# A Mamba stage and a 4-bit feed-forward stage on one core: sums of W_out for two time blocks moved in among the last scans

## The chip, the cores and the metric

The kernel runs on one core of one Trainium2 chip. The metric is the time of one execution on the device, in microseconds (us). The engines are named as the profile names them: PE multiplies matrices (its weight loads are PEld), DVE and POOL work on vectors, ACT computes functions and copies, SP only starts DMA transfers. PE sums into PSUM, which has eight banks of 128 x 512 float32; everything else lies in SBUF.

## What is computed

The input x has 8192 tokens of 512 features. Cut to what matters here:

```python
h = _layernorm(x) * (1 + ca) + sa
x = x + ga * mamba(h)                  # ends in: y = (scan + xc * D) * silu(z);  return y @ W_out.T
h = _layernorm(x) * (1 + cb) + sb
x = x + gb * ffn(h)                    # silu(q(h) @ q(Wg).T) * (q(h) @ q(Wu).T), then q(.) @ q(W_down).T
```

Here q rounds each group of 16 numbers to a 4-bit grid with a scale of its own; 1408 is the inner width of the feed-forward part. In the Mamba part a scan runs over time for each of 1024 channels and 16 states.

## The kernel before, in words

**Two stages, one after the other.** The Mamba stage takes about the first 3780 us, the feed-forward stage the rest.

**Mamba stage.** Time is cut into NC = 16 chunks of T = 512 tokens, a chunk into NJ = 4 time blocks of 128; the 1024 channels into ND = 8 channel blocks of P = 128. Two channel blocks (DH = 2) make a "half", of which there are NH = 4. The scans set the beat: a chunk is 64 slots, a slot is one scan (L547 on DVE, 128 x 1024) for one channel block and two states. The scanned states are multiplied by C, into hc by DVE (L565) or, for 5 slots of 16, into hp by POOL (L560). PE transposes these products and adds them up in the PSUM tile y (L438, `add_y`). The pool of hc has two buffers, and so has that of hp: a new one needs the y adds of the one before last.

The other work of the Mamba stage stands beside the scans by hand: `TABLE` (L577 to L617) gives each step a time in quarters of a slot, counted from the start of its chunk. Each slot has four moments (BEGIN, MID, GAP, END), `at` files a step under a slot and a moment, and `run` issues what is filed. Order on each engine is then the order of issue (`manual_schedule`). The steps at the end of a chunk are: `gate` (L450: z times y, DVE), `gate_t` (L456: PE turns the gated z of a channel block into a PSUM tile pgt), `gate_out` (L463: ACT copies it to xc, the eight of which are the input of W_out), `out_0` and `out_1` (L469: PE sums one time block po over channel blocks 0 to 3, then 4 to 7, four matmults each, 512 columns wide), `out_keep` (L482: ACT copies po; L485: it is stored to mo, for the last chunk from ACT's queue). For all chunks but the last these steps lie in the next chunk's slots; for the last one they come after all scans, in a plain loop over the slots that are left.

In PSUM the stage has a pool "mm" (one tile of one bank; pgt and po both live there), "cv" (one bank, used by the convolution), "y" (one tile of two banks) and "da" (two tiles of two banks): all eight banks.

**Feed-forward stage.** It goes by blocks of 512 tokens (n), each with four "heads" of 128 tokens. `load` (L963, L965) fetches mo and x of a head; the x tiles (h_t) have four buffers, so that of head 4 waits for PE's turn of head 0. `head` does the norm (POOL adds at L976, DVE L28 to L37, POOL L981 and L982) and the rounding to 4 bits (DVE L71 to L79, ACT L83 and L85, DVE L89 to L92, POOL L97). `turn` (PE L1002, ACT L1010) transposes a head into xqT. `up` (L1043) makes the gate and up products pg and pu, 11 pairs for each block, with L1048 (ACT), L1049 and L1050 (DVE) behind; it needs the turns of all four heads. `quantize` rounds their result, back through L1063. `down` (L1077) multiplies by W_down, and L1083 and L1084 finish a head. During the first two blocks, the four row blocks of W_down (wraw) are rounded too (`quantize_down`), transposed by PE (L1002) and copied by ACT into wd (L1033).

For the first two blocks of this stage no order is written by hand: the framework's scheduler puts the instructions of every engine in an order of its own, and it takes in what the Mamba stage left open (the tail's instructions are ordered together with the heads'). From the third block on the order is written by hand again.

Of the kernel before, what the change touches and what calls it, by code (L numbers as in the profile page):

```python
# [8 lines left out]
F32 = mybir.dt.float32  # L9
# [4 lines left out]
PSUM = bass.MemoryType.PSUM  # L14
DRAM = bass.MemoryType.DRAM

P = 128
# [91 lines left out]
def mamba_then_fp4_ffn(  # L109
# [25 lines left out]
    ND = DI // P  # L135
    NF = FF // P
    T = 512
    NJ = T // P
    NC = L // T
    NH = 4  # L140
    DH = ND // NH
# [28 lines left out]
    with ExitStack() as ma:  # L170
# [24 lines left out]
        SLOT_C = NH * SLOT_S  # L195
        NSLOT = NC * SLOT_C
        hT, xcs, bcd, dbcs, deltas, dus, zs, ys, bct, xts, pend = ({} for _ in range(11))
# [4 lines left out]
        def at(slot, moment, fn, *args):  # L202


            events.setdefault((slot, moment), []).append((fn, args))

        def run(slot, moment):
            for fn, args in events.pop((slot, moment), ()):
                fn(*args)

        pools = {}

        def run_all(slot):
            for moment in range(4):
                run(slot, moment)

        def mm_tile(name):
            return pools["mm"].tile([P, T], F32, tag="mm", name=name)
# [232 lines left out]

        def gate_t(k, d):
            h, i = divmod(d, DH)
            pg = mm_tile(f"pgt_{k}_{h}_{i}")
            for j in range(NJ):
                nc.tensor.transpose(  # L456
                    pg[:, j * P : (j + 1) * P], zs[k, h][:, j, i * P : (i + 1) * P], ident
                )
            pend["pg", k, h, i] = pg
# [2 lines left out]
            h, i = divmod(d, DH)  # L462
            nc.scalar.activation(xcs[k, h * DH + i], pend.pop(("pg", k, h, i)), AF.Copy)  # L463

        def out_mm(k, j, half):
            if half == 0:
                pend["po", k, j] = mm_tile(f"po_{k}_{j}")
            for d in range(half * (ND // 2), (half + 1) * (ND // 2)):
                nc.tensor.matmul(  # L469
                    pend["po", k, j], lhsT=xcs[k, d][:, j * P : (j + 1) * P], rhs=w_o[:, d, :],  # L470
                    start=(d == 0), stop=(d == ND - 1),
                )

        def out_0(k, j):
            out_mm(k, j, 0)

        def out_1(k, j):
            out_mm(k, j, 1)

        def out_keep(k, j):  # L480
            po = xp.tile([P, DM], F32, tag="x", name=f"po_{k}_{j}")
# [52 lines left out]
        def unit(slot):  # L534
# [90 lines left out]
            "skip": (skip_act, skip),  # L625
            "gate": (gate,),
            "gate_t": (gate_t, gate_out),
            "out": (out_0, out_1, out_keep),
        }
        for k in range(NC):  # L630
            for name, fns in steps.items():
                if k == 0 and name in ("norm", "conv", "x_proj"):
                    continue
                for m, times in enumerate(TABLE[name]):
                    for fn, time in zip(fns, times):
                        if k == 1 and name == "norm":
                            time -= 4 * (6 if m > 1 else 4)
                        if k == 0 and name in ("prep", "du") and time < 0:
                            time = min(time, 4 * -3 + GAP)
                        slot, moment = divmod(time, 4)  # L640
                        at(k * SLOT_C + slot, moment, fn, k, m)

# [2 lines left out]
        with tc.tile_pool(name="modp", bufs=1, side="right") as mp, tc.tile_pool(  # L647
            name="rawp", bufs=3, side="right"
        ) as rp, tc.tile_pool(name="qp", bufs=2, side="right") as qp, tc.tile_pool(
            name="xnp", bufs=3, side="right"  # L650
        ) as xnp, tc.tile_pool(name="qsm", bufs=3, side="right") as qsm, tc.tile_pool(
            name="p1", bufs=1, space=PSUM
        ) as p1, tc.tile_pool(name="p2", bufs=2, space=PSUM) as p2, tc.tile_pool(
            name="p3", bufs=3, space=PSUM
# [7 lines left out]
            class Work:  # L662


                @staticmethod
                def tile(shape, dtype, tag, name):
                    full = (xnp if tag == "xn" else qp).tile([P, 2 * DM], dtype, tag=tag, name=name)
                    return full[:, : shape[1]]
# [172 lines left out]
            for d in range(ND):  # L841
                h = 7 + 5 * d // 2
# [11 lines left out]
            for n, idx in enumerate((2, 5, 3, 4)):  # L854
                h = 8 + 6 * n
# [17 lines left out]
        own = dict(reuse_waits="tile")  # L873
        with ExitStack() as sa_:
# [10 lines left out]
            last = max(events)[0]  # L885
# [15 lines left out]
                    for moment in (MID, GAP, END):  # L901
                        run(slot, moment)

        for slot in range(NSLOT, last + 1):
            run_all(slot)
        order.close()


# [3 lines left out]
    with ExitStack() as fa:  # L912
# [261 lines left out]
        for n in range(2, NQ):  # L1174
# [3 lines left out]
            for q in range(NS):  # L1178
# [6 lines left out]
                else:  # L1185
                    f = q if q < split else q - NJ
                    c, i = divmod(f, FPB)
# [61 lines left out]
```

## Time and profile before

| what | us |
|---|---|
| median of 3 runs | 5715.73 |
| lowest and highest run | 5714.27, 5717.09 |
| the profiled execution | 5718.11 |
| its span in the trace | 5716.0 |
| PE busy | 5229.2 (91%) |
| DVE busy | 4963.9 (87%) |
| POOL busy | 4049.8 (71%) |
| ACT busy | 3215.3 (56%) |

Times below are counted from the start of the span of the profiled execution. A row of the timeline gives start, length, engine, line, operation, output and inputs, their sizes, and how many instructions (x) it holds; in brackets stands how long the engine had been idle before it, and what ended that. A matmult of 512 columns leaves two records, so x8 is four matmults. The granted clock is the share of its full speed that PE's clock was given.

### The profile page before, as it was taken

Reading aid. Unit: us, or ns where it says so; the run is one execution under the profiler, and the core shown is the slowest. Engines: PE = TensorE matmul, PEld = TensorE weight load, DVE = VectorE, ACT = ScalarE, POOL = GpSimd, SP = SyncE. Lnnn points to the kernel's source line nnn. Section 1 sums busy time; section 2 is a strip of 40 time slices with the busy share of each in tenths; the row PEclk is TensorE's granted clock in tenths of the full one; section 3 lists DMA queues with packets and bytes.
Section 4 is the critical chain, followed back from the end, with each engine's and each line's share of the span. In section 5 each row is a group of like instructions: output and inputs, shape, how many; then the busy total and the mean of one; then the engine's idle time right before and its main releaser. Section 6 shows DMA issues by size and latency. Waiting matters only on the chain. (4 is left out here: it accounts for less than half of the span.)

```text
span 5716.0 us, 59762 instructions
## 1 busy us (share of the span) xinstructions
PE 5229.2 (91%) x19844; PEld 3067.9 (54%) x19844; DVE 4963.9 (87%) x4003; ACT 3215.3 (56%) x7319; POOL 4049.8 (71%) x2548
## 2 busy tenths in 40 slices
PE   7789889889899898898998998778999999999999
PEld 4566565556565565565666655543444444444444
DVE  7899999999999999999999999988688788877885
ACT  6677786777777777777777776632122212221221
POOL 4899999999999999999999999973222233223320
PEclk9899999999999999999999999889999999999999
DMA  5444454454544444445445444540100010000100
GB/s 182 150 157 158 159 161 155 154 167 153 166 156 156 158 154 160 160 161 159 162 153 163 155 157 152 162 157 13 33 32 23 24 33 30 24 24 30 33 13 15
DMA packets 221996, 659.50 MB, mean 115 GB/s; under 512 B 24915, under 2 KB 40403, under 8 KB 221686
## 3 DMA queue, kind: packets, MB, share of 16 engines
q1 hardware_dynamic: 221110, 654.63, 35.2%
q8 instruction: 156, 2.56, 0.2%
q14 instruction: 154, 1.26, 0.1%
q10 hardware_dynamic: 576, 1.05, 0.0%
HBM read 615.22 MB, written 40.38 MB: 115 GB/s over the span
## 5 line engine op out<-in xcount | busy, mean ns | idle before, releaser
L509 POOL TENSOR_TENSOR db<-bc,du 128x1022 f32<-128x1022 f32 x1024 | 2388.7, 2356 | 26.6 <-DVE da L547 22.6
L547 DVE TENSOR_TENSOR_SCAN da<-da,db 128x1024 f32<-128x1024 f32 x704 | 1609.9, 2287 | 101.0 <-ACT da L522 89.2
L522 ACT ACTIVATE da<-delta,na 128x512 f32<-128x512 f32 x2048 | 1412.3, 690 | 90.1 <-DVE hp L547 62.1
L565 DVE TENSOR_TENSOR hc<-da,bc 128x1024 f32<-128x1024 f32 x704 | 861.3, 1223 | 95.3 <-PE y L438 46.0
L438 PE MATMUL y<-ident,hc 128*128 128x128 f32 x5632 | 766.9, 286 | 162.4 <-DVE hc L565 106.5
L438 PEld LDWEIGHTS y<-ident,hc 128*128 128x128 f32 x5632 | 672.9, 147 | 340.1 <-DVE hc L565 159.8
L97 POOL TENSOR_TENSOR xn<-xn,sc 128x1536 f32<-128x1536 f32 (+2 forms) x80 | 199.8, 2497 | 859.9 <-DVE xn L92 852.5
L560 POOL TENSOR_TENSOR hp<-hp,bc 128x1024 f32<-128x1024 f32 x320 | 754.0, 2356 | 25.6
L547 DVE TENSOR_TENSOR_SCAN hp<-da,db 128x1024 f32<-128x1024 f32 x320 | 730.0, 2281 | 44.4 <-ACT da L522 38.7
L1043 PE MATMUL pu<-xqT,wu 128*128 128x512 f32 x1408 | 635.6, 594 | 10.0 <-DVE g L1049 10.0
L1043 PE MATMUL pg<-xqT,wg 128*128 128x512 f32 x1408 | 635.3, 593 | 1.2 <-ACT xqT L1010 0.7
L83 ACT ACTIVATE a<-xn 128x512 f32<-128x512 f32 (+2 forms) x144 | 145.7, 1012 | 871.7 <-DVE xn L79 834.9
L1077 PE MATMUL po<-wd,hT 128*128 128x512 f32 x1408 | 609.8, 594 | 2.0 <-DVE hT L1063 2.0
L280 PE MATMUL cv<-hT,w_in 128*128 128x512 f32 x1024 | 498.7, 633 | 32.2 <-ACT hT L273 16.0
L412 PE MATMUL pz<-w_in,hT 128*128 128x256 f32 x2048 | 497.9, 399 | 27.3 <-DVE z L427 22.0
L308 PE MATMUL cv<-raw,taps 128*128 128x512 f32 x1024 | 467.9, 600 | 5.6 <-ACT taps L294 5.1
L469 PE MATMUL po<-w_o,xc 128*128 128x512 f32 x1024 | 463.2, 598 | 4.0 <-ACT po L482 3.3
L412 PEld LDWEIGHTS pz<-w_in,hT 128*128 128x128 f32 x2048 | 405.5, 203 | 97.4 <-DVE z L427 26.4
L1043 PEld LDWEIGHTS pu<-xqT,wu 128*128 128x128 f32 x1408 | 267.6, 191 | 347.0 <-issue 324.3
L545 ACT ACTIVATE state<-da 128x2 f32<-128x2 f32 x703 | 118.1, 168 | 595.6 <-DVE hc L565 594.4
L1077 PEld LDWEIGHTS po<-wd,hT 128*128 128x128 f32 x1408 | 268.5, 191 | 340.5 <-issue 331.4
L1043 PEld LDWEIGHTS pg<-xqT,wg 128*128 128x128 f32 x1408 | 265.2, 190 | 322.6 <-issue 316.2
(125 smaller groups left out, 6709.0 us busy)
## 6 DMA issues: line engine op xcount, KB each, us to landing
bc<-bc SPq DMA_DIRECT2D x1024, 512.0 KB, 4.4
x<-in_x_dram SPq DMA_DIRECT2D x64, 256.0 KB, 4.7
h<-in_x_dram SPq DMA_DIRECT2D x64, 256.0 KB, 3.0
x<-mo SPq DMA_DIRECT2D x64, 256.0 KB, 2.9
out_dram<-x SPq DMA_DIRECT2D x64, 256.0 KB, 2.0
mo<-po SPq DMA_DIRECT2D x60, 256.0 KB, 2.2
w_in<-in_w_inT_dram SPq DMA_DIRECT2D x2, 2048.0 KB, 9.0
wm<-in_wmod_dram SPq DMA_DIRECT2D x8, 512.0 KB, 4.7
```

What stands on the lines that cost most here:

```text
L280: nc.tensor.matmul(ps, lhsT=w_in[:, f, o : o + P], rhs=hT[k][:, f, :], start=(f == 0), stop=(f == NK - 1),)
L308: nc.tensor.matmul(v, lhsT=taps[:, i, :], rhs=raw[:, i : i + T], start=(i == 0), stop=(i == 3))
L412: nc.tensor.matmul(pz[:, b, :], lhsT=hT[k][:, f, t0 : t0 + P], rhs=w_in[:, f, o : o + DH * P], start=(b == 0 and f == 0), stop=(f == NK - ...
L438: nc.tensor.matmul(y[:, j, i * P : (i + 1) * P], lhsT=src[:, j * P : (j + 1) * P], rhs=ident, start=start and j % 2 == 0, stop=stop, is_tr ...
L469: nc.tensor.matmul(pend["po", k, j], lhsT=xcs[k, d][:, j * P : (j + 1) * P], rhs=w_o[:, d, :], start=(d == 0), stop=(d == ND - 1),)
L509: nc.gpsimd.tensor_tensor(db[:, :, 1:], bct[slot // DH, 0][:, :, 1:], dus[k, h, i][:, 1:].unsqueeze(1).to_broadcast([P, GN, T - 1]), ALU.mult,
L522: nc.scalar.activation(pend["da", slot][:, q, :], deltas[k, h][:, i, :], AF.Exp, scale=na[:, d, n : n + 1])
L547: nc.vector.tensor_tensor_scan(flat(to), flat(da), flat(db), 0.0, ALU.mult, ALU.add)
L560: nc.gpsimd.tensor_tensor(to, to, c_rows, ALU.mult)
L565: nc.vector.tensor_tensor(hc, hs, c_rows, ALU.mult)
L1043: nc.tensor.matmul(ps, lhsT=wt[:, k, f * P : (f + 1) * P], rhs=xqT[n][:, k, :], start=(k == 0), stop=(k == NK - 1),)
L1077: nc.tensor.matmul(pos[j], lhsT=hTs[n, c][:, o : o + P], rhs=wd[:, f0 + i, :], start=(f0 + i == 0), stop=(f0 + i == NF - 1),)
```

## The change

It has three parts.

- For the last chunk, the sums of time blocks 0 and 1 over channel blocks 0 to 5 (six matmults each) are issued beside the last scans: `out_early`, at times 222 and 230 of the last chunk, which are the moments GAP of slots 55 and 57. After the gate of the last half, `out_1` adds the two channel blocks that are left; `out_0` does nothing for these two. Time blocks 2 and 3 keep their eight matmults behind the gate.
- For the last chunk, the odd time blocks take the tile of the pool "cv" in place of that of "mm".
- The two last turns of gated z (channel blocks 6 and 7 of the last chunk) take tiles of a new PSUM pool "plast" with two buffers, which is open only during the loop over the slots after the scans. The banks are those of "da", which is closed by then.

```diff
         def gate_t(k, d):
             h, i = divmod(d, DH)
-            pg = mm_tile(f"pgt_{k}_{h}_{i}")
+            if k == NC - 1 and h == NH - 1:
+                pg = pools["last"].tile([P, T], F32, tag="mm", name=f"pgt_{k}_{h}_{i}")
+            else:
+                pg = mm_tile(f"pgt_{k}_{h}_{i}")
...
-        def out_mm(k, j, half):
-            if half == 0:
-                pend["po", k, j] = mm_tile(f"po_{k}_{j}")
-            for d in range(half * (ND // 2), (half + 1) * (ND // 2)):
+        def out_mm(k, j, blocks):
+            if blocks[0] == 0:
+                tile = cv_tile if k == NC - 1 and j % 2 else mm_tile
+                pend["po", k, j] = tile(f"po_{k}_{j}")
+            for d in blocks:
...
+        def early(k, j):
+            return k == NC - 1 and j < 2
+
+        def out_early(k, j):
+            out_mm(k, j, range(ND - DH))
+
         def out_0(k, j):
-            out_mm(k, j, 0)
+            if not early(k, j):
+                out_mm(k, j, range(ND // 2))

         def out_1(k, j):
-            out_mm(k, j, 1)
+            out_mm(k, j, range(ND - DH if early(k, j) else ND // 2, ND))
...
+        for j, time in enumerate((222, 230)):
+            at((NC - 1) * SLOT_C + time // 4, time % 4, out_early, NC - 1, j)
...
-        for slot in range(NSLOT, last + 1):
-            run_all(slot)
+        with tc.tile_pool(name="plast", bufs=2, space=PSUM, **own) as pools["last"]:
+            for slot in range(NSLOT, last + 1):
+                run_all(slot)
```

In the changed kernel the order of the instructions in the first two blocks of the feed-forward stage is another one too, since the scheduler orders them together with the tail. On PE, all 20 matmults that are left of W_out stand ahead of the turns of heads 0 to 3; before, these turns stood between time blocks 0 to 3. On DVE, the scales of the first two row blocks of W_down stand ahead of the norms of heads 4 to 7; before, they stood behind them. On SP, the loads of these two row blocks stand ahead of those of heads 4 to 7. On PE, the turn of head 8 stands behind three matmults of the first `down`, that of head 9 behind the eight after these; before, both stood ahead of all of it. The Mamba stage is otherwise in the same order, and so is all that comes after.

## The prediction

> **What bounds the kernel now.** I read the page's busy shares and slices first, then the sums by stretch, then the matmults (PE) and the waits around the place where the Mamba stage (up to about 3784 us) ends and the feed-forward stage begins.
>
> ```profile
> PE 5229.2 (91%) x19844; PEld 3067.9 (54%) x19844; DVE 4963.9 (87%) x4003; ACT 3215.3 (56%) x7319; POOL 4049.8 (71%) x2548
> ...
> PE   7789889889899898898998998778999999999999
> ...
> DVE  7899999999999999999999999988688788877885
> ```
>
> DVE stands at nine tenths to the end of the scans (slice 26 of 40), PE from there on; between them lie two slices in which neither is full.
>
> ```profile
> 3740.00:3784.00 44.00, 22.99 (x130) 20.38 (x128) 42.62 (x34) 19.14 (x44) 40.38 (x25) 0.72 0.59 190
> 3784.00:3826.40 42.40, 36.97 (x86) 16.51 (x84) 29.75 (x54) 12.01 (x20) 24.45 (x22) 0.84 0.61 217
> 3826.40:3987.60 161.20, 133.36 (x341) 62.30 (x342) 144.35 (x162) 48.69 (x61) 64.92 (x36) 0.93 0.06 19
> 3987.60:5716.00 1728.40, 1722.78 (x4168) 773.71 (x4167) 1338.20 (x1569) 362.45 (x442) 473.15 (x329) 1.00 0.08 26
> ```
>
> These are stretch, length, then busy PE, PEld, DVE, ACT, POOL, and the granted clock. In the last 44 us of the scans DVE is full (42.62) and PE half empty (22.99). In the last row PE is idle for 5.6 us of 1728: whatever brings PE to 3987.6 earlier comes out at the end whole, and nothing else does. So the question is when the turn of head 8 (pt of h_8, L1002) and what follows it can run, which before is at 3985.45.
>
> ```profile
> 3754.04 1.86 PE L438 MATMUL y<-ident,hc 128*128 128x128 f32 x8 [4.17 <-DVE hc L565]
> ...
> 3763.26 1.97 PE L438 MATMUL y<-ident,hc 128*128 128x128 f32 x8 [4.61 <-DVE hc L565]
> ...
> 3786.69 9.63 PE L469 MATMUL po<-w_o,xc 128*128 128x512 f32 x16 [0.69 <-ACT xc L463]
> 3799.58 10.01 PE L469 MATMUL po<-w_o,xc 128*128 128x512 f32 x16 [3.26 <-ACT po L482]
> 3809.43 0.82 PE L1002 MATMUL pt<-ident,h 128*128 128x128 f32 x6
> 3810.27 7.13 PE L469 MATMUL po<-w_o,xc 128*128 128x512 f32 x16
> 3817.24 0.82 PE L1002 MATMUL pt<-ident,h 128*128 128x128 f32 x6
> 3818.09 7.13 PE L469 MATMUL po<-w_o,xc 128*128 128x512 f32 x16
> 3825.07 0.60 PE L1002 MATMUL pt<-ident,h 128*128 128x128 f32 x4
> 3826.40 3.70 PE L1043 MATMUL pg<-xqT,wg 128*128 128x512 f32 x8 [0.74 <-ACT xqT L1010]
> ```
>
> Time blocks 0 to 3 of W_out run one after the other (x16 is one block: a 512-column matmult is two records). Between them stand the turns of heads 0 to 3, although POOL (L97) had these heads ready at 3803.35, 3805.82, 3810.79 and 3813.26. The first up product waits for the last of them: here PE is late, by 3825.07 − 3813.26 = 11.8 us.
>
> ```profile
> DVE am L71 <- POOL h L982: 11.2, 7, 2.7
> DVE e L89 <- ACT e L85: 5.8, 3, 3.5
> DVE hT L1063 <- POOL xn L97: 2.9, 3, 1.2
> DVE st L28 <- POOL x L976: 2.6, 1, 2.6
> ```
>
> These are DVE's largest waits in 3782 to 3990 (us, times, longest). From 3826 to 3987 it is DVE that leads (144.35 of 161.20; PE waits 27.84 there). By stretch DVE is idle 5.2 us (3782.43 to 3812.06, heads 0 to 3), 10.4 (3812.06 to 3838, heads 4 to 7 starting, each step in turn with POOL) and 13.9 (3838 to 3984.37): 29.5 in all.
>
> **The change part by part.** Numbers of instructions and transfers stay: 64 records of L469, the same copies, the same bytes. What changes is order, and the order of the first two blocks of the feed-forward stage is chosen by the scheduler, so it changes too. I walked the changed order by hand with the durations of these rows.
>
> *Early blocks.* Six matmults each for time blocks 0 and 1 go behind the y adds that end at 3749.87 and behind two groups of y adds after that. One costs 0.858 us at full clock (8 records take 3.43 us), six 5.15. Block 0 takes 3749.87 to 3755.0; the y adds (x8 and x8) to 3756.8; block 1 to 3761.9; the adds of the hc made at 3756.28 (1.09) end at 3762.8 or so. That hc's buffer, one of two, is wanted by the hc at 3765.52: 2.7 us to spare. The idle gaps of 4.17 and 4.61 hide them; cost 0. The sums stay in the mm and cv tiles until the gate, and nothing else of the last chunk asks for these any more. Without the cover they would cost 10.3 us.
>
> *Other tiles for the last turns of z, and for odd time blocks.* The second turn (pgt) no longer waits for the first one's copy: the wait of 0.69 at 3784.89 goes, xc_7 comes 0.8 sooner. The 3.26 (po on the copy of po) goes: block 2's tile was copied out while block 1's two matmults run. New waits: none.
>
> *PE's tail.* 20 matmults instead of 32: 17.2 us at full clock, about 2.5 more for the half clock up to 3791.74 (granted clock by stretches). Block 3 ends at about 3806 instead of 3825.1. All of it now stands ahead of the turns of heads 0 to 3; heads 0 and 1 may wait to 3806, which delays nothing, since the first up product needs all four. Head 3 is there at 3813.26, still; from its turn to the first up product the rows show 3826.40 − 3825.07 = 1.33. So that product starts at 3814.6: **11.8 us earlier**. The other 7 us of the tail's 19 are lost to the wait for head 3, which hangs on the end of the scans.
>
> *What DVE makes of it.* In the new order, DVE does the scales of W_down's rows 0 and 1 (L71, L73, L75, L77) right after head 3, ahead of the norms of heads 4 to 7; before they came after them. SP loads these rows ahead of the inputs of heads 4 to 7, and the load of h_4, which had waited for PE's turn of h_0 (SP's waits: 31.0 us in three, the longest 18.6), may go at 3806. One row's scales take 1.61 + 0.20 + 0.69 + 2.27 = 4.77, two 9.5 us, and their data is there: they fill the stretch in which DVE had idled 10.4. In my walk 3.5 us of idling are left there (1.1 for x of head 4, which POOL adds behind head 3; 2.4 for the first g, L1049); the 13.9 after it stay, in other places (head 6 and 7's L71 among them). 5.2 + 3.5 + 13.9 = 22.6 against 29.5: **−6.9** for the turn of h_8, at 3978.6. Bounds: 0, if heads 4 to 7 start that much later, and −10.4, if the hole closes. I take −6.9, since POOL's and DVE's steps for heads 4 to 7 still alternate. So PE's lead of 11.8 is partly waited away, most of it at the turns of heads 4 to 7.
>
> *Three matmults ahead.* Before, PE idled 4.69 ahead of the turn of h_8, with all 88 of down's records after it. Now three matmults of down (L1077) stand before it in PE's queue: 3 × 0.858 = **−2.6**, in that idle time. Bounds: 0 and −2.6.
>
> [...] L91 (xn, 512 wide) takes 0.69 alone and 2.96 at 3858.74 beside POOL's L97; L77 is 2.27 in the row I used. [...]
>
> **Sum.** 0 − 6.9 − 2.6 = −9.5. The profiled execution took 5718.11 (span 5716.0, 2.1 around it): 5708.6. It lies 2.4 above the median of the runs, 5715.73: **5706.2**.
>
> **Rivals.**
> *A, the forecast*: −9.5, give or take 2.5. Chance 0.60.
> *B, the chain of DVE and POOL at heads 4 to 7 does not move*: these start only from POOL's L976 after head 3 (3813.32 before), and the scales put ahead of their norms delay them as much as they fill. For it: 11.2 us of DVE's waits are for POOL's L982. Against it: that chain's DVE steps are 0.7 us each, and it waits for POOL far more than POOL for it. Only the three matmults are left: −2.6, 5713.1; with half of the hole −5, 5710.7. Chance 0.16.
> *C, PE's lead is carried whole*: −11.8 − 2.6 = −14.4, 5701.3. For it: the scales were the work that held the later turns of W_down (PE waits 8.1 for the copy of wd). Against it: DVE is busy 144 of 161 us there. Chance 0.18.
> *D, the end of the scans moves, slower*: the early matmults run at half clock, 10.3 us a block. Then 3749.87 + 10.3 + 3.8 (y adds at half clock) + 10.3 + 1.9 = 3776.2 for the adds that free the buffer of the hc at 3765.52: DVE waits 10.7, the scans end 10.7 later, and all behind them. −9.5 + 10.7 = +1.2, 5716.9; with B +8.1, 5723.8. It decides from the point where both blocks take over 2.7 us longer than at full clock. For it: the clock was granted at half in 3754.20 to 3757.61 and 3761.02 to 3781.50. Against it: those stretches follow PE's idle gaps, which the blocks fill. [...] Chance 0.06.
>
> **How the numbers follow.** A measurement of this kernel can tell about 0.2%, 11.4 us, from no change. Faster by more (below 5704.3): C 0.18 and the far side of A 0.08, 0.26. Slower by more: a part of D, 0.02. Within it: 0.72. The range takes in A's width, C less its far end, and the better half of B: 5700.0 to 5712.0.
>
> **What would show it.** Early blocks: L469 rows x12 near 3750 and 3757, no wait of DVE for PE y L438 there, the last scan within 0.5 us of before. Tail: 40 records of L469, gone by 3806; first L1043 at 3814 to 3815. DVE: L71 on wraw near 3812, idle from there to 3838 about 3.5. Turn of h_8 at 3978 to 3979 behind six records of L1077. The stretch behind as long as before. It is wrong if DVE idles as long as before around heads 4 to 7, if the scans end later, or if PE's waits after 3988 grow beyond 5.6 us.

## The result and the profile after

The changed kernel takes 5706.47 us (median of 19 runs, 5694.64 to 5710.39) against 5714.48 for the kernel before (19 runs, 5709.52 to 5723.0). The ratio is 0.9982, 95% interval 0.9976 to 0.9989: faster by 6 to 14 us. The forecast was 5706.2, 9.5 us below the 5715.73 from which it counted; the two medians here lie 8.0 us apart.

The profiled execution took 5694.64 us (span 5692.8), 23 us less than the profiled one before. That is more than the change: the two traces must be cut where the scans end. The last gate of z (DVE L450) begins at 3782.43 before and at 3771.07 after. The first scan of the last chunk already begins at 3563.55 and 3552.20; the stretch from there to the gate, the only part of the scans that the change touches, takes 218.88 and 218.87. So **11.4 us of the 23 arose ahead of the first moved instruction**, and *The change again* below shows that they are a difference between executions.

The rest is read behind the gate. The yardstick from here on is the time from that gate to DVE's add of head 4 (the fifth row of the line that adds down's sum to x): 4105.50 − 3782.43 = 323.1 us before, 4083.66 − 3771.07 = **312.6** after. All adds from head 4 to head 59 but one (10.1) show the same difference, 10.5 us. The last three show 12.2. That last part is not put down to the change: from the add of head 59 to that of head 63 it takes 41.8 us before and 40.1 after, but 40.1 too in before_late_load (below), whose code there is that of before.

The page after, then the sums by stretch, cut at the same places as before (end of the scans, first up product, turn of head 8):

```profile
PE 5215.7 (92%) x19844; PEld 3069.1 (54%) x19844; DVE 4960.3 (87%) x4003; ACT 3214.1 (56%) x7319; POOL 4052.6 (71%) x2548
...
PE   7789889899899898998998988778999999999999
...
DVE  7899999999999999999999999998687788877885
```

```profile
3728.60:3772.60 44.00, 29.43 (x154) 21.80 (x153) 42.61 (x34) 19.17 (x45) 40.41 (x25) 0.84 0.57 191
3772.60:3803.80 31.20, 22.15 (x63) 10.55 (x62) 25.87 (x43) 10.68 (x19) 17.10 (x16) 0.84 0.80 285
3803.80:3966.90 163.10, 136.05 (x340) 63.77 (x340) 146.22 (x172) 51.50 (x64) 75.09 (x42) 0.91 0.06 21
3966.90:5692.80 1725.90, 1719.88 (x4168) 773.43 (x4168) 1336.38 (x1570) 360.13 (x441) 472.79 (x331) 1.00 0.08 26
```

DVE's busy time beside the last scans is what it was (42.61 against 42.62), PE's rose from 22.99 to 29.43, at a granted clock of 0.84 instead of 0.72. The second stretch shrank from 42.4 to 31.2, the third grew by 1.9, the last shrank by 2.5.

From the last gate to the turn of head 8, before and after:

```profile
3782.43:3985.45 203.02, 168.85 (x420) 77.36 (x420) 173.52 (x217) 60.10 (x80) 88.55 (x58) 0.92 0.18 61
3771.07:3966.97 195.90, 158.79 (x404) 74.71 (x404) 173.69 (x218) 62.18 (x82) 92.31 (x57) 0.90 0.19 63
```

DVE is busy for as long as before (173.52 and 173.69 us), so the 7.1 us by which the turn comes earlier are idle time of DVE (29.5 us before, 22.2 after). From there to the add of head 4 PE has no idle time in either kernel, and this part takes 120.05 us before and 116.69 after, since four matmults of `down` now stand ahead of the turn.

PE's timeline, the same places:

```profile
3738.35 5.32 PE L474 MATMUL po<-w_o,xc 128*128 128x512 f32 x12
3743.50 1.04 PE L438 MATMUL y<-ident,hc 128*128 128x128 f32 x8
3744.38 1.04 PE L438 MATMUL y<-ident,hp 128*128 128x128 f32 x8
3745.25 5.32 PE L474 MATMUL po<-w_o,xc 128*128 128x512 f32 x12
...
3773.53 17.43 PE L474 MATMUL po<-w_o,xc 128*128 128x512 f32 x40 [0.25 <-ACT xc L467]
3792.07 0.66 PE L1019 MATMUL pt<-ident,h 128*128 128x128 f32 x4 [1.10 <-POOL h L97]
3794.53 1.12 PE L1019 MATMUL pt<-ident,h 128*128 128x128 f32 x4 [1.81 <-POOL h L97]
3799.50 1.12 PE L1019 MATMUL pt<-ident,h 128*128 128x128 f32 x4 [3.85 <-POOL h L97]
3801.98 1.11 PE L1019 MATMUL pt<-ident,h 128*128 128x128 f32 x4 [1.36 <-POOL h L97]
3803.78 5.63 PE L1060 MATMUL pg<-xqT,wg 128*128 128x512 f32 x8 [0.69 <-ACT xqT L1027]
```

The early blocks run at a granted clock of 1.00 (3738.35 to 3750.57; 12 records in 5.32 us), the 20 matmults that are left in one piece, and now PE waits for each head: the turns have moved from 27.0, 27.4, 35.0 and 42.6 us behind the gate to 21.0, 23.5, 28.4 and 30.9. The first up product comes 32.7 behind it instead of 44.0.

DVE's waits in 3771 to 3979:

```profile
DVE am L71 <- POOL h L999: 6.6, 5, 2.7
DVE e L89 <- ACT e L85: 4.5, 2, 2.3
DVE g L1066 <- PE pu L1060: 2.8, 2, 1.4
DVE g L1066 <- ACT e L85: 2.6, 1, 2.6
```

The wait for POOL's L999 (L982 before) fell from 11.2 to 6.6 us. By stretch behind the gate, DVE's idle time was 5.2 (to 29.6 us), 10.4 (to 60), 1.5 (to 100), 6.2 (to 135), 6.2 (to 205), and is 5.3, 2.7, 4.2, 3.2, 7.9: up to 205 us, which is past the turn of head 8, 29.5 became 23.2 (differences of rounded values). What is gone is the hole behind head 3.

### The profile page after: what moved, and what is told of

It reads as the page before. It is cut to its first block, busy times and chain, and to the rows that moved or that the text cites. A ratio compares the mean times of both kernels' runs of the same rounds, so it can differ in the third digit from the quotient of the medians.

```text
span 5692.8 us, 59765 instructions
## 1 busy us (share of the span) xinstructions
PE 5215.7 (92%) x19844; PEld 3069.1 (54%) x19844; DVE 4960.3 (87%) x4003; ACT 3214.1 (56%) x7319; POOL 4052.6 (71%) x2548
## 3 DMA queue, kind: packets, MB, share of 16 engines
q8 instruction: 156, 2.56, 0.2%
## 5 line engine op out<-in xcount | busy, mean ns | idle before, releaser
L521 POOL TENSOR_TENSOR db<-bc,du 128x1022 f32<-128x1022 f32 x1024 | 2388.6, 2357 | 23.9 <-DVE da L559 19.6
L97 POOL TENSOR_TENSOR xn<-xn,sc 128x1536 f32<-128x1536 f32 (+2 forms) x80 | 204.0, 2550 | 849.6 <-DVE xn L92 842.6
## 6 DMA issues: line engine op xcount, KB each, us to landing
w_in<-in_w_inT_dram SPq DMA_DIRECT2D x2, 2048.0 KB, 11.2
```

What stands on the lines that cost most here:

```text
L521: nc.gpsimd.tensor_tensor(db[:, :, 1:], bct[slot // DH, 0][:, :, 1:], dus[k, h, i][:, 1:].unsqueeze(1).to_broadcast([P, GN, T - 1]), ALU.mult,
```

## The experiments

Two theories stood at first: **PE's work** (the gain is the 12 matmults, 10.3 us, taken off PE's way, or the earlier first up product), and **the order** (DVE leads from head 3 to head 8, and what counts is whether its queue has work in the hole). A third, that the loads of heads 4 to 7 set the gain since they wait for PE's turns of heads 0 to 3, came up in between.

The scheduler orders the first two blocks of the feed-forward stage anew for each of these kernels, so most of them differ from the changed kernel in more than their edit. Up to the add of head 4, tiles_only and one_early have one order on DVE, and pad_tail and pad24 one on DVE, POOL and ACT. The changed kernel, tiles_only, one_early and late_load were executed several times, the others once; on the yardstick two executions of the changed kernel differ by 0.4 us.

| kernel | turn of head 0, 3 | first up | turn of head 8 | add of head 4 | DVE idle, 29.6 to 60 | DVE idle, 0 to the turn of head 8 |
|---|---|---|---|---|---|---|
| before | 27.0, 42.6 | 44.0 | 203.0 | 323.1 | 10.4 | 29.5 |
| changed | 21.0, 30.9 | 32.7 | 195.9 | 312.6 | 2.7 | 22.2 |
| changed, again | 21.0, 30.9 | 32.7 | 195.6 | 312.2 | 2.5 | 21.8 |
| tiles_only | 31.6, 33.6 | 34.9 | 198.3 | 315.3 | 5.1 | 24.5 |
| one_early | 24.9, 30.9 | 32.7 | 197.5 | 314.9 | 2.9 | 22.5 |
| plast_only | 26.5, 34.8 | 47.2 | 194.6 | 315.3 | 6.8 | 23.9 |
| pad_tail | 30.0, 31.9 | 33.2 | 195.8 | 312.0 | 2.9 | 19.6 |
| pad_up | 21.0, 30.9 | 45.0 | 191.9 | 312.4 | 3.0 | 21.3 |
| pad24 | 40.3, 42.2 | 43.5 | 205.3 | 321.6 | 14.9 | 33.5 |
| late_free | 21.0, 30.9 | 45.1 | 192.7 | 312.4 | 4.1 | 23.0 |
| dve_more | 21.0, 30.9 | 32.7 | 201.9 | 317.1 | 4.6 | 16.9 |
| late_load | 20.3, 30.2 | 32.0 | 185.4 | 304.9 | 5.8 | 18.6 |
| late_tiles | 32.3, 34.2 | 35.6 | 192.2 | 311.8 | 10.8 | 22.8 |
| before_late_load | 26.8, 42.5 | 49.4 | 197.6 | 321.3 | 10.7 | 29.8 |

All columns but the last two are us behind the last gate, from each kernel's trace; a turn is given by its first matmult. What is left of the turn of head 8 when the last column is taken off is DVE's busy time up to it. The gain at the add of head 4 also depends on how many matmults of `down` stand ahead of that turn: none before, four in the changed kernel.

**The change again.** No edit.

> The changed kernel as it is, again. All theories: from the last gate of z to the add of head 4 312.6 us within 1. The question is the scans: in the two profiles they ended 11.4 us earlier in the changed kernel than before, though nothing of the change stands ahead of the last nine slots. If that is a difference between executions and not the change's, the scans' end lies elsewhere in this profile (3771 in the first one, 3782 before), by several us; if it is the change's, it is at 3771 again within 2.

Measured: 312.2, and the scans' end at 3785.60 instead of 3771.07, with the same code. So the 11.4 us in the scans are a difference between executions; the time behind the gate repeats within 0.4. Median 5709.16 of 12 runs, 10.8 us below the kernel before in the same set; ratio 0.9979 (0.9969 to 0.9989).

**Without the early blocks (tiles_only).**

```diff
         def early(k, j):
-            return k == NC - 1 and j < 2
+            return False
...
-        for j, time in enumerate((222, 230)):
+        for j, time in ():
```

> The changed kernel without its early blocks: the last turns of z keep the new tiles, the odd time blocks keep the cv tile, but all 32 matmults of the last chunk's W_out stand behind the gate. Measured is the time from the last gate of z to DVE's add of head 4 (before 323.1 us in its profile, the changed kernel 312.6), because the time of the scans ahead of it differs by up to 11 us between executions of the same code. Theory, gate to the order: the two new tiles and the order of the feed-forward start that comes with them bring most of the gain; 12 matmults more (10.3 us) on PE push the first up product from 32.7 us behind the gate to about 36, and DVE, not PE, sets what follows, so the add of head 4 comes at 315 to 316.5, a gain of 6.5 to 8 of the 10.5. Rival, PE's work: the 10.3 us taken off PE are the gain, so without them the add comes at 322 to 323, as before. In time: theory about 7 us under before, rival within 1 us of it.

Measured: 315.3, a gain of 7.8 of the 10.5; ratio 0.9984 (0.9975 to 0.9992). All 32 matmults stand behind the gate again and three quarters of the gain are there. So the 12 early matmults bring at most a quarter of what the change is worth.

**One early block (one_early).**

```diff
         def early(k, j):
-            return k == NC - 1 and j < 2
+            return k == NC - 1 and j < 1
...
-        for j, time in enumerate((222, 230)):
+        for j, time in enumerate((222,)):
```

> The changed kernel with only the first of the two early blocks (six matmults for time block 0), time block 1 whole behind the gate: 26 matmults there instead of 20. Theory: six matmults take 5.15 us and PE's tail ended some 11 us ahead of head 3 in the changed kernel, so the first up product does not move (32.7 us behind the gate, at most 0.5 later) and the add of head 4 stays at 312.6, give or take 0.7: the second early block is worth nothing. Rival, PE's work: half of the early work, half of its gain, the add at 317 to 318. In time: theory as the changed kernel, rival 5 us above it.

Measured: the first up product at 32.7, as expected, but the add at 314.9: a miss by 1.6 us past the bound of my expectation. The turns of heads 2 and 3, the first up product and the norms of heads 4 to 6 (36.1, 37.3, 38.6) come when they do in the changed kernel, so it is not PE's tail. Set side by side in the traces, DVE's order from 42 to 77 us and from 87 to 115 us behind the gate is another one than in the changed kernel, and it is exactly that of tiles_only, which ends within 0.4 us of this kernel. That the 2.3 us come from this choice of the scheduler fits, but it was only read off, not tried; the ratio of times, 0.9985 (0.9976 to 0.9994), can't tell that from the changed kernel.

**The new tiles for the last turns of z alone (plast_only).** As tiles_only, and:

```diff
-                tile = cv_tile if k == NC - 1 and j % 2 else mm_tile
+                tile = mm_tile
```

> The kernel before with one part of the change, the new PSUM tiles for the two last turns of gated z; all time blocks of W_out go through the one mm tile, none is early. PE again has turns of heads between time blocks, but ends them sooner. Theory, turns and loads: the last of the turns of heads 0 to 3 comes at 33 to 36 instead of 42.6, head 4's input not before 25; the add of head 4 at 316 to 319, half or more of the gain from this one tile, even if the first up product stays at 44 or later. Rival, PE's work or PE's lead: no gain without an earlier first up product, 322 to 323 or later.

Measured: 315.3, better than expected, with the first up product 3.2 us later than before the change. A gain of 7.8 with a later first up product: its time says nothing here. The expectation missed one thing: the turn of head 3 begins at 34.8, but its second half stands at 42.1, hardly sooner than before (42.6). And in this kernel the scales of W_down's row 0 begin at 54.9, as before the change (55.0): **three quarters of the gain come without the scales in the hole**. In the hole, the norm of head 5 moved from 39.9 to 33.3, directly behind that of head 4. Up to the turn of head 8, DVE is idle 5.6 us less than before and has 2.8 us less work ahead of it.

**PE's work put back, in two places.** Twelve unread matmults ahead of the turns (pad_tail) and twice as many (pad24):

```diff
             out_mm(k, j, range(ND - DH if early(k, j) else ND // 2, ND))
+            if k == NC - 1 and j == NJ - 1:
+                spare = pools["last"].tile([P, T], F32, tag="mm", name="spare")
+                for d in range(12):      # 24 in pad24
+                    nc.tensor.matmul(
+                        spare, lhsT=xcs[k, d % ND][:, :P], rhs=w_o[:, d % ND, :],
+                        start=(d == 0), stop=(d == 11),
+                    )
```

and twelve behind the turns (pad_up):

```diff
+        spare = pdn.tile([P, DM], F32, tag="po", name="spare")
+        for d in range(12):
+            nc.tensor.matmul(
+                spare, lhsT=wg[:, d % NK, :P], rhs=xqT[0][:, d % NK, :],
+                start=(d == 0), stop=(d == 11),
+            )
         NQ = L // T
```

> The changed kernel with 12 matmults more (10.3 us) at the same place, between the last time block of W_out and the turns of heads 0 to 3: as much PE work behind the gate as before the change. Theory: turns at 31 to 34 instead of 21 to 31, first up product at about 34, so the add of head 4 at 312 to 315: nearly all of the gain stays, though the work that the early blocks took off PE's tail is back. Rival, PE's work: 322 to 323.

> The changed kernel with 12 matmults more (512 columns each, about 10.3 us) on PE, behind the turns of heads 0 to 3 and ahead of the first up product; nobody reads their sum. Turns stay at 21 to 31 us behind the gate, the first up product moves from 32.7 to about 43.5, which is where it stood before the change (44.0). Theory, turns and loads: what counts is that PE's turns of heads 0 to 3 free the input buffers of heads 4 to 7 (four buffers), so that their loads and norms come early; DVE leads after that, PE has 27 us of waits to lose there, and the add of head 4 stays at 312 to 314. Rival, PE's lead: the gain is the earlier first up product, so it goes, and the add of head 4 comes at 322 to 323 as before the change.

> The changed kernel with 24 matmults more (about 20.6 us) on PE, between the last time block of W_out and the turns of heads 0 to 3; nobody reads their sum. These turns move to 41 to 44 us behind the gate (before the change they stood at 27 to 43), the first up product to about 44 to 45; the order of DVE's work with W_down's scales ahead stays that of the changed kernel. Theory, turns and loads: the inputs of heads 4 to 7 come 12 to 20 us later than in the changed kernel, and the add of head 4 comes at 320 to 324, the whole gain gone. Rival, DVE's order: the scales standing in the hole behind head 3 are the gain whatever PE does, the add of head 4 at 313 to 316.

Measured: 312.0, 312.4 and 321.6. With 10.3 us of PE work added in either place the gain stands whole, though DVE's order is another one than in the changed kernel from about 40 us behind the gate on. pad_up's first up product is 1 us later than before the change:

```profile
3803.77 1.12 PE L1019 MATMUL pt<-ident,h 128*128 128x128 f32 x4 [1.36 <-POOL h L97]
3805.57 12.49 PE L1132 MATMUL spare<-xqT,wg 128*128 128x512 f32 x24 [0.69 <-ACT xqT L1027]
3817.90 3.60 PE L1060 MATMUL pg<-xqT,wg 128*128 128x512 f32 x8
```

Most of the work went into PE's waits: between 60 and 100 us behind the gate PE is idle for 11.8 us in the changed kernel (one wait, for ACT's copy of wd) and for 2.4 in pad_up. In pad24 only 1.5 us of the gain are left, and DVE's waits in 3807.9 to 3840.3 say where:

```profile
DVE st L28 <- POOL x L1000: 10.6, 1, 10.6
DVE g L1073 <- PE pu L1067: 3.9, 1, 3.9
```

Head 4's norm stands next in DVE's queue, and its input, loaded only once PE has turned head 0 (here at 40.3), is late. The norm of head 4 in pad_tail, then in pad24:

```profile
3821.41 0.69 DVE L28 BATCH_NORM_STATS2 st<-x 128x6 f32<-128x512 f32 x1
3823.24 0.69 DVE L28 BATCH_NORM_STATS2 st<-x 128x6 f32<-128x512 f32 x1 [10.62 <-POOL x L1000]
```

Behind their gates (3785.33 and 3778.27) these are 36.1 and 45.0 us. Since the two kernels share their order on DVE, POOL and ACT, the 9.5 us between them come from twelve matmults on PE, nearly all of their 10.3 us. So in this order PE's work ahead of the turns costs nothing up to pad_tail's length, where the norm of head 4 still has other DVE work ahead of it, and nearly its full length from there to pad24, where this norm waits for its input, which fitted the theory of turns and loads.

**Loads of heads 4 to 7 held back (late_free).** As pad_up, and behind the twelve matmults:

```diff
+        for t in range(NJ):
+            nc.tensor.transpose(spare[:, t * P : (t + 1) * P], firsts[t][:, :P], ident)
```

with `firsts` the tiles of heads 0 to 3, so that their buffers stay taken.

> The kernel of pad_up (12 matmults that nobody reads ahead of the first up product, the gain intact at 312.4) with one thing more: behind these matmults PE transposes 128 columns of each of heads 0 to 3 once more, into the same unread sum. So the turns stay at 21 to 31 us behind the gate, but the buffers of heads 0 to 3 come free only at about 44, and the loads of heads 4 to 7 with them. Theory, turns and loads: these loads set the gain, the add of head 4 comes at 319 to 323. Rival, DVE's queue: what counts is whether DVE finds other work in that time (the rounding of W_down's rows stands ready there, and the scheduler puts the norms of heads 4 to 7 behind it, since it knows that they come late); then the add of head 4 stays at 311 to 314 although the norms start 13 us later.

Measured: 312.4. The norm of head 4 begins 49.7 us behind the gate instead of 36.1, and nothing is lost. DVE's timeline in the place of the hole:

```profile
3816.03 2.70 DVE L77 TENSOR_SCALAR sc<-sc,gc 128x88 f32<-128x88 f32 x1
3818.65 1.61 DVE L89 SCALAR_TENSOR_TENSOR e<-a,e 128x1408 f32<-128x1408 f32 x1
3820.30 0.89 DVE L90 TENSOR_SCALAR e<-e 128x1408 uint32<-128x1408 uint32 x1
3821.30 1.63 DVE L91 SCALAR_TENSOR_TENSOR xn<-e,xn 128x1408 f32<-128x1408 f32 x1
3822.96 1.62 DVE L92 SCALAR_TENSOR_TENSOR xn<-e,xn 128x1408 f32<-128x1408 f32 x1
3826.18 2.62 DVE L89 SCALAR_TENSOR_TENSOR e<-a,e 128x1408 f32<-128x1408 f32 x1 [1.60 <-ACT e L85]
3829.95 0.69 DVE L28 BATCH_NORM_STATS2 st<-x 128x6 f32<-128x512 f32 x1 [1.16 <-POOL x L993]
```

The scheduler put the rounding of W_down's rows (1408 wide) ahead of the norms that come late, so DVE's queue was full. The theory of turns and loads falls as stated: a late load cost time where DVE's queue had it at its head (pad24), and none here, where the scheduler had put other work ahead of it.

**More work for DVE in the hole (dve_more).**

```diff
+        for _ in range(again):           # 3 for W_down's row blocks 0 and 1, else 1
-        nc.vector.tensor_reduce(am, blocks(src), AX.X, ALU.max, apply_absolute_value=True)
+            nc.vector.tensor_reduce(am, blocks(src), AX.X, ALU.max, apply_absolute_value=True)
```

> The changed kernel with four more maxima on DVE: L71 is done three times instead of once for each of W_down's row blocks 0 and 1 (same result), 4 x 1.61 = 6.4 us more in the stretch behind head 3, where DVE is idle for 2.7 us after the change. Theory, DVE leads from head 3 to head 8: 2.7 us at most are hidden there, the add of head 4 comes 4 to 6 us later, at 316.5 to 318.5. Rival, PE leads (its waits are only the price of its order): the add of head 4 stays within 1.5 us of 312.6.

Measured: 317.1. Of 6.4 us added to DVE, 4.5 come out at the end, although PE has 37.2 us of idle time up to the add of head 4 here, as in the changed kernel (37.1). This is what DVE in the lead would do. It is no clean measure of it, since the order changed too: up to the turn of head 8 DVE is busy 11.3 us longer than in the changed kernel and idle 5.3 us less.

**W_down's rows 0 and 1 behind the norms of heads 4 to 7 (late_load).**

```diff
-        load_down(0)
...
-        load_down(1)
...
-        todo += quantize_down(0)
-        todo += quantize_down(1)
...
                     beside(*(head((n + 1) * NJ + j) for j in (2 * c, 2 * c + 1)))
+                if n == 0 and c == 1:
+                    for r in range(2):
+                        load_down(r)
+                        todo += quantize_down(r)
```

> The changed kernel, but the loads and the rounding of W_down's row blocks 0 and 1 are issued after the norms of heads 4 to 7, so their scales no longer stand in the stretch behind head 3 where DVE had idled before the change. The prediction's step said that these scales there are worth 6.9 us. Theory as predicted: DVE idles 10 us again around heads 4 to 7, and the add of head 4 comes at 319 to 320. Rival, the scales are in the way there: heads 4 to 7 start 9 us sooner without them, their turns come 15 us or more sooner, and the W_down rounding finds room later in waits that are there anyway; the add of head 4 comes at 303 to 310, earlier than in the changed kernel.

Measured: 304.9, 7.7 us better than the changed kernel; 5706.13 us, ratio to before 0.9972 (0.9961 to 0.9983). My step's reason falls here: with the scales out of the hole DVE idles 5.8 us in it, not 10, and the end comes earlier. Heads 4 to 7 now fill part of the hole, since they start together. The turn of head 8 comes 10.5 us earlier than in the changed kernel: DVE has 6.9 us less work ahead of it (busy 166.8 against 173.7) and is idle 3.7 less. 2.9 of this are lost again behind the turn, where no matmult of `down` stands ahead. So most of this gain is work that moved behind the turn. PE's waits from the first up product (3816.8) to 3971:

```profile
PE pu L1060 <- DVE g L1066: 9.2, 3, 6.7
PE pt L1019 <- POOL xn L97: 3.8, 3, 2.8
PE pt L1019 <- ACT wd L1050: 3.3, 1, 3.3
PE pt L1019 <- POOL h L97: 2.8, 1, 2.8
```

and of the changed kernel (3803 to 3967):

```profile
PE pt L1019 <- ACT wd L1050: 11.8, 1, 11.8
PE pt L1019 <- POOL xn L97: 9.6, 2, 6.0
PE pt L1019 <- POOL h L97: 5.7, 1, 5.7
```

The one wait of 11.8 behind W_down's rows shrank to 3.3. By the yardstick this is the fastest kernel of all. Its median of 7 runs lies 3.0 us below that of the changed kernel in the same set (5709.16), with intervals that overlap.

**The same edit before the change, and without the early blocks (before_late_load, late_tiles).** The edits of late_load in the kernel before, and those of late_load and tiles_only together.

> The kernel before with the edit of late_load alone: loads and rounding of W_down's row blocks 0 and 1 issued behind the norms of heads 4 to 7. In the changed kernel this edit was worth 7.7 us more. Theory: before the change the heads 4 to 7 come in one by one behind PE's turns, so moving W_down's rows away from them helps little or nothing there: the add of head 4 at 320 to 324 (323.1 before). Rival, the two edits are independent: 315.5.

> The kernel of late_load without the early blocks (as tiles_only is to the changed kernel). With W_down's rows out of the way, heads 4 to 7 stand directly behind heads 0 to 3, so a later turn of these counts more. Theory: turns 3 to 11 us later, the add of head 4 at 309 to 312, so that the early blocks are worth 4 to 7 us here against 2.7 in the changed kernel. Rival: the early blocks are worth the same 2.7 us or nothing, 305 to 308.

Measured: 321.3 and 311.8. Before the change the edit brings 1.8 of 7.7: the hole stays (10.7), for heads 4 to 7 come one by one. Without the early blocks the hole is back too (10.8), and they are worth 311.8 − 304.9 = 6.9 us here, against 2.7 in the changed kernel: where the norms of heads 4 to 7 are what DVE has next, the time of the turns counts. And late_tiles, with the hole as long as before the change, still ends 0.8 us ahead of the changed kernel: the hole alone does not set the end.

## Why the prediction was right, step by step

- **Early blocks, cost 0: right.** The last chunk's scans take 218.87 against 218.88; between executions this stretch differs by up to 1 us (219.84 in the second one of the changed kernel, and in tiles_only, which has no early blocks). Rival D needed half clock; the blocks ran at a granted clock of 1.00 (3738.35 to 3750.57).
- **Tail and first up product, −11.8: right in size**, 44.0 − 32.7 = 11.3, with PE waiting for every head. The 20 matmults took 17.4 us and not 19.7, since the granted clock was 1.00 in 3773.5 to 3791, and ended 19.9 us behind the gate and not 23.6; this changed nothing, as PE then waited for the heads. But it is no term of the gain: pad_up gives it back entirely and loses nothing, if in another DVE order. The prediction had it as a lead "partly waited away, most of it at the turns of heads 4 to 7"; the 11.8 us wait for wd ahead of the turn of head 4 is that place.
- **DVE, −6.9: right in size.** DVE's idle time up to the turn of head 8 fell by 7.3 (29.5 to 22.2), the hole from 10.4 to 2.7 (forecast 3.5), and the turn came 203.0 − 195.9 = 7.1 earlier. **The reason was half right.** That this turn came earlier by idle time of DVE is what the two rows up to that turn show (in the result), and pad24 loses the gain with the hole open again. That the scales have to be what fills the hole is not so: plast_only has 7.8 of the 10.5 without them there, and late_load is faster without them. The size agrees in part by luck: the scales of the two rows took 8.1 us (rows of L71 to L77 from 3800.64 on) and not 9.5, and three norms stand among them.
- **Three matmults ahead, −2.6: mis-sized.** They are four. PE's rows after:

```profile
3957.66 3.60 PE L1094 MATMUL po<-wd,hT 128*128 128x512 f32 x8
3966.97 1.12 PE L1019 MATMUL pt<-ident,h 128*128 128x128 f32 x4 [5.72 <-POOL h L97]
3967.88 8.00 PE L1094 MATMUL po<-wd,hT 128*128 128x512 f32 x14
```

  Eight records, 4 × 0.858 = 3.4. With it the sum is 7.1 + 3.4 = 10.5, which is what the adds show; the step, and the text on the change ahead of it, counted three.
- **L77, taken as 2.27 us for each of the two W_down rows: too long.** Its row for the first was 1.33 after, and that for the second 0.65. A DVE operation that took longer beside POOL's L97 after the change is in the last section.
- **The time** agrees within 0.3 us, which is luck to that degree: one execution differs from the next by up to 16 us (5694.64 to 5710.39). The comparable numbers are 10.5 by the trace and 8.0 by the medians, against 9.5; both lie inside the interval 6 to 14.
- **A sign of being wrong** was that PE's waits behind the turn of head 8 grow beyond 5.6 us. They are 5.9 after; the 0.3 stand behind PE's last matmult (3.89 us to the end of the span, 3.59 before), so they are no wait.

What stays open: why the scheduler chose one DVE order for tiles_only and one_early and another for the changed kernel, whether that alone makes the 2.3 us between one_early and the changed kernel, and what in the scans differs between executions. No run keeps DVE's order of the kernel before under the changed tail, or the reverse, so the gain is not split between the earlier turns and the new order. Giving heads 4 to 7 buffers of their own was not tried.

## What to carry to other kernels

Where an engine has waits in a stretch, taking work off it can be worth nothing by itself; put the same work back beside it (pad_tail, pad_up) and see whether the time moves, then put back more (pad24) to find where it begins to count. Look for the engine whose idle time in the stretch changed, and ask what stands at the head of its queue there: a small edit ahead of a part that a scheduler orders is worth what the new order is worth. late_load and the changed kernel have the same instructions on every engine, and this part differs by 7.7 us. And cut a trace where the edit begins, before reading a gain off its span.

## What the runs showed of the hardware

Executions of one program differ in the Mamba stage: the last gate of z began at 3771.07 and 3785.60 in two executions of the changed kernel, while the time from there to the add of head 4 repeated within 0.4 us. And one very small DVE operation took longer beside POOL: in the changed kernel, L73 (32 columns) takes 0.17 us at 3786.93, with no POOL instruction beside it, but 2.56 here, to the end of POOL's L97 that had begun before it (3825.06 + 3.97 = 3829.03):

```profile
3826.51 2.56 DVE L73 TENSOR_SCALAR sc<-am 128x32 f32<-128x32 f32 x1
3828.99 0.67 DVE L71 TENSOR_REDUCE am<-h 128x32 f32<-128x512 f32 x1
```

```profile
3825.06 3.97 POOL L97 TENSOR_TENSOR xn<-xn,sc 128x1408 f32<-128x1408 f32 x1
```

L71, next in DVE's order, begins as L97 ends and takes 0.67 us, as it does at 3823.13. No run tried what holds L73 here.
